# One table of 516-value rows for layer 1 of a two-layer graph attention kernel

## The chip, the cores and the metric

The kernel runs on one core of a Trainium2 chip. The metric is the device time of one execution in microseconds (us); the kernel before has a median of 4654.79 us over 3 runs (4652.91 to 4660.41). A profile was taken of a further execution.

## The reference

The inputs are 6250 nodes with 256 values each (`x`), 200,000 edges sorted by destination (`src`, `dst`) with 32 attributes each, and two layers of weights. Before the layers, each node row is normalized (`_layernorm`) and clipped at zero. One layer does the following, cut to what matters (`_gat`; `_add_self_loops` adds one edge from each node to itself, with the mean of its incoming edge features):

```python
te = relu(edge_attr @ We + be) * exp(x @ Wo + bo)[src][:, None]
hx = (x @ Wg).reshape(n, h, f)
al = leaky_relu(einsum(hx, a_s)[src] + einsum(hx, a_d)[dst] + einsum(he, a_e), 0.2)
al = exp(al - segment_max(al, dst)[dst])
al = al / segment_sum(al, dst)[dst]
out = segment_sum(hx[src] * al[:, :, None], dst) + b
```

Layer 0 has 4 heads, layer 1 has 1 head. Layer 0 is followed by a residual and a relu, layer 1 by residuals. So layer 1 needs, for any edge, the row of its source node as layer 0 left it, and layer 0 is complete only after its last edges.

## The kernel before, in words

**Steps.** The edges are cut into chunks of 128 and the chunks into 66 steps per layer (`NS`): 64 steps of 24 chunks, and two shorter ones. A step holds edges in order of destination, so its destinations are a window of at most 112 consecutive nodes (`M`), starting at a row known only at run time. The 132 steps run in one stream, unrolled, by `edges`; the last three steps of a layer are interleaved by hand in `ending`, which also starts the next layer. That place is called the turn here, and the last three steps of layer 0 are called a, b and c.

**One step.** GpSimd (POOL) issues 24 indirect DMAs (`gathers`, L1116). Each brings 128 source rows, one per partition, from the node table of the layer into a buffer `G`; there are three such buffers, so a step's gathers can start once the sums of three steps before are done. TensorE turns edge attributes into logits (`y`, `zad`); VectorE (DVE) computes logits, running maxima and weights, scales `G` (L1517), builds one-hot rows `S` (L1346); TensorE then adds up the 24 chunks into the window's nodes (`sums`, L1529: 24 products `S`ᵀ`G`, each recorded as two matmuls). `evict` (L1535) copies the sum out on ScalarE (ACT), and one to two steps later `finish`, `rows1`, `rows2` and `rows3` complete the window's nodes while the next sums run.

**Node tables.** Layer 0 gathers from `T[0]`, written in the prologue. A finished window of layer 0 gives rows `trow` of 516 values: 260 that layer 1 gathers (`L1.TW`), and 256 that layer 1 adds to its output at the end (`D`). The kernel before writes them to up to three places: the 260 values to `T[1]` (L1662), for the gathers of layer 1; for all steps before a, the same 260 values again to `T1e` (L1664); and all 516 values to a fixed place in `nd` (`rows4`, L1687), from which layer 1 loads a window's rows as `tw` (`nodes`, L1184). As a step's first node may be shared with the step before, `rows4` also patches one value in the other `nd` table (L1690).

**The turn.** While a, b and c still finish, the gathers of the first step of layer 1 already run (`early_rows` in `ending`): they read `T1e`, which holds all rows written before a. Rows that were missing then are the last 256 nodes at most. `lack_rows` loads those from `T[1]` after the stores of a, b and c (L1317), and `complete` adds them to the gathered chunks by a product with a selection matrix (L1333) on TensorE, and one VectorE operation per chunk (L1335).

**What sets the order.** SyncE's queue (SP) issues nearly all other DMAs, in program order: loads of edge attributes (`ea`), local indices (`lb`), flags (`fl`) and node rows (`tw`), and all stores. An SP instruction that waits holds up all behind it. A store to an address known only at run time is tracked as covering its whole table, so a store to `T[1]` waits until the one before has landed, a load waits for stores before it in program order, and a store waits for earlier reads. A run-time address is read by `row` with a TENSOR_LOAD into an SP register.

Of the kernel before, what the change touches and what calls it, by code (L numbers as in the profile page):

```python
# [31 lines left out]
P = 128  # L32
# [49 lines left out]
class Kernel:  # L82
# [10 lines left out]
    def run(self):  # L93
        nc, tc = self.nc, self.tc
        self.cp = self.pool("consts")
        self.dp = self.pool("tables", space=DRAM)
        N = self.N
        self.T = [self.dp.tile([N + P, L.TW], F32, name=f"T{L.l}") for L in self.L]
        self.T1 = self.dp.tile([N + P, self.L[1].TW], F32, name="T1e")
        n, w = (self.NS + 1) // 2, self.L[1].TW + D  # L100
        self.nd = [self.dp.tile([n * (M + 1), w], F32, name=f"nd{i}") for i in range(2)]
        self.x1 = self.dp.tile([N + P, D], F32, name="x1")
        with ExitStack() as c:
            c.enter_context(tc.manual_schedule())
            self.gp = [self.pool("gath0", 1, c)]
            self.ps_k = self.pool("ps_k", 1, c, space=PSUM)
            self.lp = self.pool("loads", 2, c)
            self.sp, self.wp, self.xp = (self.pool(n, b, c, side="right") for n, b in (("onehot", 2), ("work", 2), ("index", 1)))
            self.offs = offs = np.concatenate([[0], np.cumsum(self.cs)]).tolist()
            self.steps = [dict(L=L, s=s, C=self.cs[s], o=offs[s], k=L.l * self.NS + s)  # L110
                          for L in self.L for s in range(self.NS)]
            self.prologue(c)
            self.edges(c)
        self.general()
# [793 lines left out]
    def ending(self, a, b, c, pv, late, after):  # L908
# [197 lines left out]
    def gathers(self, st, behind=None):  # L1106
        nc, L = self.nc, st["L"]
        own, G = "own" in st, st.get("own")
        if not own:
            G = self.G0 if st["k"] == 0 else self.gp[st["k"] % 3].tile([P, C, 270], F32, name="G")  # L1110
        st["G"] = G
        idx = self.src[:, st["o"]:st["o"] + st["C"]]
        last = st["C"] - 1
        c0 = (self.CX, self.CX1, 0)[min(st["k"], 2)]
        for i, c in enumerate(range(last + 1) if own else (last, *range(c0, last)) if c0 <= last else ()):
            g = nc.gpsimd.indirect_dma_start(  # L1116
                out=G[:, c, 0:L.TW], out_offset=None, in_=st.get("from", self.T[L.l])[0:self.N, :],
                in_offset=bass.IndirectOffsetOnAxis(ap=idx[:, c:c + 1], axis=0))
            self.after_product(g, behind(i) if behind else None)
            yield  # L1120
# [57 lines left out]
    def nodes(self, st):  # L1178
        nc, L, s = self.nc, st["L"], st["s"]
        tw = self.tws[st["k"] % 4]  # L1180
        st["tw"], st["xw"] = tw[:, :L.TW], tw[:, L.TW:L.TW + D]
        if L.l:
            n = s // 2 * (M + 1)
            nc.sync.dma_start(tw[1:M + 1, :L.TW + D], self.nd[s % 2][n:n + M, :])  # L1184
            return
        st["r"] = r = self.row(0, s)
# [63 lines left out]
    def lacking(self):  # L1250
# [4 lines left out]
        for n in (N - 2 * P, N - P):  # L1255
            nc.sync.dma_start(self.T1[n:n + P, :], none)
        first = self.base_f[:, NS - 3:NS - 2]
# [54 lines left out]
    def lack_rows(self, st):  # L1312

        st["tail"] = [self.np_.tile([P, 272], F32, name="U", bufs=3) for _ in range(2)]
        for j, t in enumerate(st["tail"]):
            n = self.N - 2 * P + P * j
            self.nc.sync.dma_start(t[:, :self.L[1].TW], self.T[1][n:n + P, :])  # L1317

# [337 lines left out]

    def rows3(self, st):
        nc, L, s = self.nc, st["L"], st["s"]
        if L.l == 0:
            self.table_row(st)  # L1660
            r, t, L1 = st["r"], st["trow"], self.L[1]
            nc.sync.dma_start(self.T[1][ds(r, M), :], t[1:M + 1, :L1.TW])  # L1662
# [11 lines left out]
        elif s < self.direct:  # L1674
            r = self.row(1, s)
            nc.sync.dma_start(out[ds(r, M), :], o[1:M + 1, :])
# [7 lines left out]
    def rows4(self, st):  # L1684
        nc, s, t, L1 = self.nc, st["s"], st["trow"], self.L[1]
        n = s // 2 * (M + 1)
        nc.sync.dma_start(self.nd[s % 2][n:n + M, :], t[1:M + 1, :])  # L1687
        if s:
            n = self.row(2, s - 1)
# [11 lines left out]
    def general(self):  # L1701
# [4 lines left out]
        with tc.If(fl == 0):  # L1706
            with ExitStack() as c:
# [3 lines left out]
                nc.vector.memset(zero, 0.0)  # L1711
                nc.sync.dma_start(self.T[1][N:N + P, :], zero[:, :self.L[1].TW])
                for L in self.L:
                    self.general_layer(L, wp, pp)

    def general_layer(self, L, wp, pp):
# [71 lines left out]
        def nodes(n0):  # L1788
# [8 lines left out]
            if l == 0:  # L1797
# [3 lines left out]
                self.table_row(st)  # L1801
                nc.sync.dma_start(self.T[1][rows, :], st["trow"][:, :self.L[1].TW])
                nc.sync.dma_start(self.x1[rows, :], st["trow"][:, self.L[1].TW:])
# [103 lines left out]
```

## Time and profile before

| | |
|---|---|
| median of 3 runs | 4654.79 us |
| the profiled execution's own time | 4678.05 us |
| its span, first to last instruction | 4676.0 us |
| busy: TensorE matmul (PE) | 2921.0 us, 62% |
| busy: VectorE (DVE) | 2837.0 us, 61% |
| busy: ScalarE (ACT) | 534.2 us, 11% |
| busy: GpSimd (POOL) | 3002.6 us, 64% |
| mean granted TensorE clock | 0.748 |
| share of 16 DMA engines: gathers (software queue), the other DMAs of SP | 34.4%, 11.0% |
| read from HBM, written | 544.23 MB, 45.36 MB |

Times are read from the start of the span. "L1116" is line 1116 of the kernel before. In a timeline row the first column is the start, the second the duration, and the brackets at the end say how long the engine was idle ahead of it and what ended that; "issue" means that it waited for nothing that the profile shows, "remote" that the releaser isn't known. Matmul ends are modelled, so the row of a sum tells when it was issued rather than when its result stood.

### The profile page before, as it was taken

The numbers are of one execution on the slowest core, as the hardware profiler recorded it, in microseconds if no ns is written. First come the engines' busy times: TensorE is split into PE (matmuls) and PEld (weight loads), VectorE is DVE, ScalarE is ACT, GpSimd is POOL, SyncE is SP. The second block draws the span as 40 slices with busy tenths as digits, with TensorE's granted clock in tenths as the row PEclk, the third lists the DMA queues.
The fourth block names the chain that finished last, engine by engine and source line by source line (L and its number), as shares of the span: only waits on it lengthen the run. The fifth ranks groups of instructions, "written<-read, shape, count | busy, mean of one in ns | idle before, by whom it ended". The sixth has DMA issues, their size and how long they took to land.

```text
span 4676.0 us, 35049 instructions
## 1 busy us (share of the span) xinstructions
PE 2921.0 (62%) x10090; PEld 1845.5 (39%) x10090; DVE 2837.0 (61%) x6222; ACT 534.2 (11%) x1189; POOL 3002.6 (64%) x3201
## 2 busy tenths in 40 slices
PE   8766666655666656656665566566565565656656
PEld 6533433433434433433443334334343343333434
DVE  7767666666667666666675555455554554545546
ACT  5211111111111111111110000000000000000000
POOL 5566666666666666666656666666666666666664
PEclk9877777777777777778787766767767777676777
DMA  7344444444544444544444444444444444444442
GB/s 228 109 124 130 138 126 130 138 125 131 140 125 132 136 127 132 140 125 131 133 125 114 125 114 122 124 121 118 118 124 119 118 126 112 121 125 114 122 123 74
DMA packets 248234, 591.77 MB, mean 127 GB/s; under 512 B 65849, under 2 KB 105125, under 8 KB 247783
## 3 DMA queue, kind: packets, MB, share of 16 engines
q0 software_dynamic: 150048, 422.51, 34.4%
q1 hardware_dynamic: 97009, 164.82, 11.0%
q10 hardware_dynamic: 976, 2.12, 0.1%
q8 instruction: 81, 1.33, 0.1%
q14 instruction: 120, 0.98, 0.1%
HBM read 544.23 MB, written 45.36 MB: 126 GB/s over the span
## 4 chain that ended last, share of the span: by engine, by line
DVE 25%; PE 22%; issue 21%; POOL 19%; another core or an unknown queue 10%; DMA 1%; ACT 1%; DVEq 0%; POOLq 0%; ACTq 0%
POOL G L1116 18%; PE u L1529 15%; DVE G L1517 10%; DVE S L1346 3%; PE y L1218 3%; DVE lb L1242 1%; DMA G<-T,src 1%; DVE m L1467 1%; PE fin L587 1%; DVE rt L1395 1%; PE ps L587 1%; PE zad L1227 1%; DVE al L1413 1%; PE fin L1621 1%
## 5 line engine op out<-in xcount | busy, mean ns | idle before, releaser
L1116 POOL DMA_INDIRECT G<-T,src x3066 | 2931.1, 956 | 1574.2 <-issue 896.3
L1529 PE MATMUL u<-G,S 128*128 128x270 f32 (+1 forms) x6212 | 1716.8, 434 | 792.8 <-issue 567.0
L1529 PEld LDWEIGHTS u<-G,S 128*128 128x128 f32 x6212 | 1316.7, 214 | 1124.8 <-issue 609.9
L1517 DVE TENSOR_TENSOR G<-G,kps 128x6144 f32<-128x6144 f32 (+6 forms) x152 | 854.5, 5629 | 0.0
L1218 PE MATMUL y<-ea,webd 64*128 64x256 f32 (+2 forms) x1056 | 450.4, 805 | 341.1 <-issue 326.8
L1445 DVE TENSOR_TENSOR_SCAN cl<-fl,cl,lf 4x129 f32<-4x129 f32 (+1 forms) x130 | 61.1, 470 | 858.1 <-remote 730.6
L1346 DVE TENSOR_TENSOR S<-kps,loc 128x3072 f32<-128x3072 f32 (+2 forms) x136 | 438.2, 3222 | 4.6
L1227 PE MATMUL zad<-R,wea 128*64 128x384 f32 (+1 forms) x1056 | 291.7, 691 | 160.9 <-ACT R L1219 104.7
L1218 PEld LDWEIGHTS y<-ea,webd 64*128 64x128 f32 x1056 | 159.9, 284 | 493.1 <-issue 472.9
L1535 ACT ACTIVATE U<-u 128x270 f32<-128x270 f32 (+1 forms) x130 | 51.2, 394 | 1953.9 <-remote 1485.5
L1219 ACT ACTIVATE R<-y,webd 128x1024 f32<-128x1024 f32 (+3 forms) x264 | 235.6, 892 | 325.2 <-PE y L1218 166.5
L1227 PEld LDWEIGHTS zad<-R,wea 128*64 128x64 f32 x1056 | 84.5, 180 | 415.7 <-ACT R L1219 221.1
L1413 DVE TENSOR_TENSOR al<-G 128x96 f32<-128x96 f32 (+1 forms) x132 | 34.3, 260 | 240.4 <-remote 198.5
L1395 DVE STREAM_TRANSPOSE rt<-zad 128x768 f32<-128x768 f32 (+1 forms) x130 | 125.9, 968 | 24.0 <-remote 20.4
L587 PE MATMUL fin<-wg,h1T 128*128 128x260 f32 x264 | 122.8, 613 | 1.5 <-issue 1.1
L1435 PE MATMUL lf<-ident,fb 128*36 128x128 f32 (+1 forms) x132 | 46.5, 353 | 120.5 <-issue 80.9
L1367 PE MATMUL zad<-a,Q 128*128 128x12 bf16 (+1 forms) x132 | 24.3, 184 | 153.6 <-issue 117.2
L1242 DVE TENSOR_TENSOR lb<-lb,kps 128x1536 bf16<-128x1536 bf16 (+1 forms) x68 | 113.0, 1661 | 0.0
L1621 PE MATMUL fin<-ident,fb 128*128 128x128 f32 x132 | 45.6, 395 | 95.4 <-issue 94.7
L1621 PEld LDWEIGHTS fin<-ident,fb 128*128 128x128 f32 x132 | 25.2, 194 | 166.0 <-issue 163.6
L1560 ACT ACTIVATE mw<-mw,mg 128x2 f32<-128x2 f32 x66 | 19.7, 298 | 595.2 <-DVE mw L1556 469.7
L1399 DVE TENSOR_REDUCE ade<-rt 128x96 f32<-128x288 f32 (+1 forms) x132 | 44.2, 335 | 70.2 <-remote 35.3
(267 smaller groups left out, 2310.1 us busy)
## 6 DMA issues: line engine op xcount, KB each, us to landing
ea<-in_ea_dram SPq DMA_DIRECT2D x64, 768.0 KB
G<-T,src POOLq DMA_INDIRECT x3066
lb<-locrow SPq DMA_DIRECT2D x64, 384.0 KB
nd<-t1rows SPq DMA_DIRECT2D x66, 225.8 KB
tw<-nd SPq DMA_DIRECT2D x66, 225.8 KB
tw<-T SPq DMA_DIRECT2D x66, 117.2 KB
T<-t1rows SPq DMA_DIRECT2D x66, 113.8 KB
tw<-in_x_dram SPq DMA_DIRECT2D x66, 112.0 KB
```

The lines of the kernel that those rows point to most:

```text
L587: self.product = self.nc.tensor.matmul(ps[:, :L.MW], hT[:, k, :], self.wg[L.l][:, k, :], start=(k == 0), stop=(k == 1))
L1116: g = nc.gpsimd.indirect_dma_start(out=G[:, c, 0:L.TW], out_offset=None, in_=st.get("from", self.T[L.l])[0:self.N, :], in_offset=bass.Indi ...
L1218: nc.tensor.matmul(y[:, i, :n], self.webd[l][r, :], ea[r, w], start=True, stop=True)
L1219: nc.scalar.activation(R[:, :, w], y[:, :, :n], AF.Relu, bias=self.be[l])
L1227: nc.tensor.matmul(st["zad"][i * PH:(i + 1) * PH, o], self.wea[l][0], R[:, i, w], start=True, stop=False)
L1242: V.tensor_tensor(lb[:, :, :n], lb[:, :, :n], self.k_part.unsqueeze(2).to_broadcast([P, i, n]), op=OP.is_equal)
L1346: nc.vector.tensor_tensor(st["S"][:, c0:c1, :], self.k_iota.unsqueeze(1).to_broadcast(w), self.loc[:, o + c0:o + c1].unsqueeze(2).to_broad ...
L1395: V.transpose(rv[:, :32 * c].rearrange("p (b n) -> p b n", b=2), z.rearrange("p (b n) -> p b n", b=2)[:, :, :16 * c])
L1413: V.tensor_add(zv, gr, G[:, :c, L.p:L.p + H])
L1517: nc.vector.tensor_tensor(v, v, pw[:, c0:c1, :].unsqueeze(3) .to_broadcast([P, c1 - c0, H, L.F]), op=OP.mult)
L1529: p = nc.tensor.matmul(st["u"][:, :L.W], S[:, i, :], G[:, i, 0:L.W], start=(j == 0), stop=(j == c - 1))
L1621: st["turned"] = self.nc.tensor.transpose(pT[:, i * P:(i + 1) * P], st["x1"][:, i * P:(i + 1) * P], self.ident)
```

## The change

`T[1]` becomes a table with rows of 516 values. `T1e` is gone.

- In layer 0, a step before a to c stores all 516 values of a window to `T[1]` in one DMA (`store_row`), except that `nd` is still written for the last four steps of the layer, which read it in layer 1. The copy to `T1e`, the store to `nd` and its patch are gone for the others.
- Gathers of layer 1 read the first 260 values of a 516-value row; there are as many of them, in the same order, with 260 values each.
- In layer 1, the first 62 steps load `tw` from `T[1]` at the window's row; the row is read into a register there and used again for the store of the output, where it was read before.
- The early gathers read `T[1]` itself. So that they see no half-written rows, a's rows are stored after the last early gather in program order; by the tracking of the whole table, this store waits until all 24 early gathers have landed. The stores of a, b and c carry 260 values each, as before.

```diff
-        self.T1 = self.dp.tile([N + P, self.L[1].TW], F32, name="T1e")
         n, w = (self.NS + 1) // 2, self.L[1].TW + D
+        self.T = [self.dp.tile([N + P, (L.TW, w)[L.l]], F32, name=f"T{L.l}") for L in self.L]
...
-            after["from"] = self.T1
...
-            self.rows3(a)
+            self.rows3(a, not early)
         self.rows1(b)
         if early:
             self.product = b["turned"]
             drain(early_rows)
+            self.store_row(a)
         self.rows2(b)
...
-        if L.l:
+        if L.l and s + 4 >= self.NS:
             n = s // 2 * (M + 1)
             nc.sync.dma_start(tw[1:M + 1, :L.TW + D], self.nd[s % 2][n:n + M, :])
             return
+        if L.l:
+            st["r"] = r = self.row(1, s)
+            nc.sync.dma_start(tw[1:M + 1, :L.TW + D], self.T[1][ds(r, M), :])
+            return
...
+    def store_row(self, st):
+        r, t, w = st["r"], st["trow"], self.L[1].TW + (0 if "lag" in st else D)
+        self.nc.sync.dma_start(self.T[1][ds(r, M), 0:w], t[1:M + 1, :w])
...
-            nc.sync.dma_start(self.T[1][ds(r, M), :], t[1:M + 1, :L1.TW])
-            if self.early and s + 3 < self.NS:
-                nc.sync.dma_start(self.T1[ds(r, M), :], t[1:M + 1, :L1.TW])
-            if "lag" not in st:
+            if store:
+                self.store_row(st)
+            if "lag" not in st and s + 4 >= self.NS:
                 self.rows4(st)
```

The order of instructions on PE, DVE, ACT and POOL is the same but for the table that the early gathers name. SP's changes. In a step of layer 0, SP's stores of the kernel before are these (the names are the destination and the source; `T1_61` is `T[1]`):

```order
L1662 DMA T1_61<-t1rows_202 112x260
L1664 ISA
L1664 DMA T1e_62<-t1rows_202 112x260
L1687 DMA nd1_64<-t1rows_202 112x516
L1175 TENSOR_LOAD base_i_1264
L1690 ISA
L1690 DMA nd0_63<-t1rows_202 1x1
```

The kernel after has one store there, and goes on to the next loads:

```order
L1142 DMA lb_9990<-locrow_1207 128x1x1536
L1142 DMA ea_10063<-in_ea_dram 128x2x768
L1663 ISA
L1663 DMA T1_61<-t1rows_201 112x516
L1174 TENSOR_LOAD base_i_1263
```

Four DMAs became one, of the size of the largest.

At the turn, SP of the kernel before issues the stores of a, b and c (L1662), the two loads of the missing rows and the first `tw` of layer 1. The names in brackets are the semaphores that the instruction waits for: DMAHW ones count DMAs of SP, DMASW ones the gathers of POOL, the others their engine.

```order
L1662 DMA T1_61<-t1rows_202 112x260 [waits DMAHW3_49,Activation_49]
L1662 ISA
L1662 DMA T1_61<-t1rows_202 112x260 [waits DMAHW4_49,DMAHW3_49,Activation_49]
L1662 DMA T1_61<-t1rows_202 112x260 [waits DMAHW5_49,DMAHW4_49,Activation_49]
L1317 DMA U_12565<-T1_61 128x260 [waits DMAHW6_49,DMAHW5_49,Pool_49]
L1317 DMA U_12566<-T1_61 128x260 [waits DMAHW7_49]
L1184 DMA tw4_203<-nd0_63 112x516 [waits DMAHW0_49]
```

In the kernel after the same place reads:

```order
L1663 DMA T1_61<-t1rows_201 112x260 [waits DMASW4_49,DMASW5_49,DMASW3_49,DMASW6_49,DMASW2_49,DMASW7_49,DMASW1_49,DMAHW4_49,DMASW0_49,Activation_49]
L1663 ISA
L1663 DMA T1_61<-t1rows_201 112x260 [waits DMAHW2_49,Activation_49]
L1663 DMA T1_61<-t1rows_201 112x260 [waits DMAHW3_49,Activation_49]
L1321 DMA U_12193<-T1_61 128x260 [waits DMAHW5_49,DMAHW4_49,Pool_49]
L1321 DMA U_12194<-T1_61 128x260 [waits DMAHW6_49]
L1174 TENSOR_LOAD base_i_1263 [waits DVE_49]
L1187 ISA
L1187 DMA tw4_202<-T1_61 112x516 [waits DMAHW7_49]
```

The first store waits for all eight semaphores of the gathers; the stores of b and c, the loads of the missing rows and the first `tw` are queued behind it.

In a step of layer 1, SP of the kernel before has the row's register load ahead of the output's store:

```order
L1184 DMA tw4_203<-nd0_63 112x516
L1143 DMA lb_14948<-locrow_1208 128x1x1536
L1143 DMA ea_15006<-in_ea_dram 128x2x768
L1175 TENSOR_LOAD base_i_1264
L1676 ISA
L1676 DMA out_0_dram<-fb_14938 112x256
```

The kernel after has it ahead of the `tw` load:

```order
L1174 TENSOR_LOAD base_i_1263
L1187 ISA
L1187 DMA tw4_202<-T1_61 112x516
L1142 DMA lb_14342<-locrow_1207 128x1x1536
L1142 DMA ea_14400<-in_ea_dram 128x2x768
L1682 ISA
L1682 DMA out_0_dram<-fb_14329 112x256
```

The register load moved from the store to the load; the number of DMAs per step is the same.

More of the change, by code (lines that the diff above doesn't have):

```diff
@@ L1116, in gathers @@
             g = nc.gpsimd.indirect_dma_start(
-                out=G[:, c, 0:L.TW], out_offset=None, in_=st.get("from", self.T[L.l])[0:self.N, :],
+                out=G[:, c, 0:L.TW], out_offset=None, in_=self.T[L.l][0:self.N, :],
                 in_offset=bass.IndirectOffsetOnAxis(ap=idx[:, c:c + 1], axis=0))
@@ L1674, in rows3 @@
         elif s < self.direct:
-            r = self.row(1, s)
+            r = st["r"] if "r" in st else self.row(1, s)
             nc.sync.dma_start(out[ds(r, M), :], o[1:M + 1, :])
```

15 lines of the change are left out of this document (7 added, 8 removed).

## The prediction

> **What bounds the kernel now.** I began with the page: the chain that ended last and the costliest groups.
>
> ```profile
> span 4676.0 us, 35049 instructions
> DVE 25%; PE 22%; issue 21%; POOL 19%; another core or an unknown queue 10%; DMA 1%; ACT 1%; DVEq 0%; POOLq 0%; ACTq 0%
> L1116 POOL DMA_INDIRECT G<-T,src x3066 | 2931.1, 956 | 1574.2 <-issue 896.3
> ```
>
> No engine holds the whole chain: VectorE, TensorE and GpSimd each have about a fifth or a quarter, and DMAs 1%. That is the mark of a loop that passes through several engines. So I took the big scaling of `G`, one per step, to count steps (its rows in two stretches, one per layer), and then the timeline of one step in the middle of layer 1.
>
> ```profile
> L1517 DVE TENSOR_TENSOR G<-G,kps x57: 6545/6545/6546, 314.6 to 2282.7; 128x6144 f32<-128x6144 f32 x57
> L1517 DVE TENSOR_TENSOR G<-G,kps x55: 6545/6545/6546, 2663.9 to 4528.2; 128x6144 f32<-128x6144 f32 x55
> 3016.14 10.83 PE L1529 MATMUL u<-G,S 128*128 128x261 f32 x48 [1.84 <-issue]
> 3040.64 0.39 ACT L1535 ACTIVATE U<-u 128x261 f32<-128x261 f32 x1 [19.99 <-remote]
> 3040.67 0.47 DVE L1445 TENSOR_TENSOR_SCAN cl<-fl,cl,lf 1x129 f32<-1x129 f32 x1 [9.91 <-remote]
> 3035.56 0.95 POOL L1116 DMA_INDIRECT G<-T,src  x1 [0.30 <-issue]
> 3040.87 0.95 POOL L1116 DMA_INDIRECT G<-T,src  x1 [4.37 <-remote]
> ```
>
> A step of layer 0 takes (2282.7 − 314.6) / 56 = 35.14 us, one of layer 1 (4528.2 − 2663.9) / 54 = 34.52 us. Within a step, 24 products start at 3016.14 and their result is copied out at 3040.64, 24.5 us later. Then, in the same third of a microsecond, VectorE leaves an idle stretch of 9.91 us and GpSimd one of 4.37 us: both waited for the sums. VectorE's serial part (maxima, weights, scaling) takes the other 34.52 − 24.5 = 10.0 us. GpSimd's 24 gathers take 24 × (0.95 + 0.30) = 30.0 us, so it has 4.4 us to spare. The loop is sums, VectorE, sums; gathers come next, 4.4 us behind. The waits say what gathers and stores cost this loop:
>
> ```profile
> PE u L1529 <- DMA G<-T,src: 16.1, 7, 3.1
> POOL G L1116 <- DMA T<-t1rows: 4.8, 1, 4.8
> PE y L1333 <- DMA U<-T: 3.9, 1, 3.9
> ```
>
> Products wait for gathered rows 16.1 us in the whole execution, in 7 places. The other two waits happen once each: at the turn.
>
> **Layer 0: four DMAs become one.** In the chain, and in the timeline of a step of layer 0:
>
> ```profile
> 2395.36 0.05 DVEq L592
> 1517.81 0.41 DVE L592 TENSOR_TENSOR t1rows<-fin,bias 128x260 f32<-128x260 f32 x1
> 1517.93 11.70 PE L1529 MATMUL u<-G,S 128*128 128x270 f32 x42 [2.83 <-DVE crow L1505]
> 1542.02 0.40 ACT L1535 ACTIVATE U<-u 128x270 f32<-128x270 f32 x1 [10.94 <-PE u L1529]
> ```
>
> About 62 steps lose the copy to `T1e`, the store to `nd` and the patch. No engine of the loop issues them, SP does. What they could hold up is the reuse of their source `t1rows`: L592 writes it at 1517.81, while the step's sums start at 1517.93 and stand at 1542.02, so VectorE has 24.1 us of cover there. The one wait that the chain shows for L592 is 0.05 us. So the term is 0; without cover it would be 0.05 us × 62 = 3 us gained. The other end is the whole difference between the layers, (35.14 − 34.52) × 62 = 38 us gained, if the stores' traffic were all of what makes a step of layer 0 longer. Layer 0 does other work in its steps (a running maximum of four heads against one, rows of the next layer), which explains a difference of 0.6 us as well, and the small share of DMA waits speaks for it. I take 0 and keep the gain as a rival.
>
> **Layer 1: gathers from wider rows.** Each gather still brings 128 × 260 values, but from rows 2064 bytes apart instead of 1040. No row of before has such a stride. The durations of all gathers so far:
>
> ```profile
> L1116 POOL DMA_INDIRECT G<-T,src x3066: 943/949/1174, 89.5 to 4630.8; - x192
> ```
>
> [...] I take 0. The other end is 1174 − 949 = 225 ns more for each, the worst that the row shows; that is a rival below. A gain here isn't excluded by a row, but GpSimd isn't the bound, so it would be worth nothing beyond the 16.1 us of landings.
>
> **Layer 1: the load of `tw`.** It now comes from `T[1]` at a run-time row, and the register is loaded ahead of it. The timeline of the same step, and the register work for the loads of layer 0, which are at a run-time row already (from the `tw` tile's rows):
>
> ```profile
> 3022.70 0.44 DVE L1643 SCALAR_TENSOR_TENSOR fb<-tw,mw,fb 128x256 f32<-128x256 f32 x1
> 3023.18 0.32 SPq L1184 DMA_DIRECT2D tw<-nd  x1
> 3026.45 0.17 DVE L1359 CAST a<-tw 128x2 bf16<-128x2 f32 x1
> L1187 SPq MOVE tw<-in_x_dram x66: 29/705/1442, 92.9 to 2337.1; - x66
> ```
>
> The load is issued when L1643 has read the place before it, 3.3 us ahead of its reader L1359. Register work ahead of such a load cost SP at most 1.4 us each (the MOVE's maximum). All of that would push L1359, the work up to the idle stretch with it, and use 1.4 of the 9.91 us that VectorE waits there anyway. So 0, with the cover named: the wait for the sums. If the cover were gone, 1.4 × 62 = 87 us; it would have to shrink seven times for that. The output's store needs its register no longer there, a gain off the path.
>
> **The turn.** Here the change adds a wait. The timeline of before around it (SP's queue, POOL, PE):
>
> ```profile
> 2398.39 11.29 SPq L1662 DMA_DIRECT2D T<-t1rows  x3
> 2406.34 0.94 POOL L1116 DMA_INDIRECT G<-T1e,src  x1 [0.30 <-issue]
> 2409.36 0.32 SPq L1662 DMA_DIRECT2D T<-t1rows  x1
> 2411.35 0.84 SPq L1317 DMA_DIRECT2D U<-T  x2
> 2412.24 0.43 SPq L1184 DMA_DIRECT2D tw<-nd  x1
> 2412.09 0.95 POOL L1116 DMA_INDIRECT G<-T,src  x1 [4.81 <-DMA T<-t1rows]
> 2413.64 0.77 PE L1333 MATMUL y<-U,G 128*128 128x260 f32 x1 [3.92 <-DMA U<-T]
> L1662 SPq EVENT_SEMAPHORE  x2: 1562/1882/2203, 2399.2 to 2402.2; - x2
> L1317 SPq EVENT_SEMAPHORE  x1: 1590/1590/1590, 2409.7 to 2409.7; - x1
> ```
>
> Before, the rows of a and b are stored from 2398.39 on, while the early gathers still run; only c's store at 2409.36 stands at the end, and has landed by 2411.3, when SP, after its wait of 1590 ns, goes on to the loads of the missing rows. After, a's store waits for the last early gather. That is issued by 2406.34 + 0.94 = 2407.28, and lands 1.6 to 2.2 us later if it takes as long as the stores (SP's waits for a store: 1562 to 2203 ns): 2408.9 to 2409.5. Behind a's store, in SP's queue, are the stores of b and c, each waiting for the one before, the loads of the missing rows, and the first `tw`. Three stores one after another, 0.33 us to issue and 1.6 to 1.9 us to land each, are 5.8 to 6.6 us: c lands at 2414.7 to 2416.1 instead of 2411.3. That is +3.4 to +4.8 us; I take the upper half, **+4.2 us**, as SP also goes through more semaphores there. Both who wait are shifted by it: PE's L1333 (its wait of 3.92 us becomes about 8.1) and GpSimd's first gather of the second step of layer 1 (4.81 becomes 9.0). Nothing hides it, as the first scaling of layer 1 needs all 24 chunks completed. The first `tw` of layer 1, at 2412.24, is shifted by as much plus at most 1.4 us; its reader L1359 comes at 2425.45, 13 us after the issue, and is shifted itself, so that stays covered.
>
> What a longer idle stretch does to the clock is the open part. Three stretches after the turn (busy time with counts of PE, PEld, DVE, ACT, POOL, then the granted clock), with rows of the timeline:
>
> ```profile
> 2413.40:2416.80 3.40, 3.16 (x7) 2.52 (x8) 2.58 (x4) 0.00 (x0) 2.79 (x3) 0.50 0.68 192
> 2416.80:2423.60 6.80, 3.90 (x18) 3.14 (x17) 3.28 (x8) 0.00 (x0) 4.97 (x6) 1.00 0.60 168
> 2423.60:2430.40 6.80, 3.90 (x12) 1.55 (x12) 1.97 (x8) 0.00 (x0) 5.28 (x6) 0.50 0.54 138
> 2425.45 0.15 DVE L1359 CAST a<-tw 128x1 bf16<-128x1 f32 x1
> 2426.23 0.16 PE L1367 MATMUL zad<-a,Q 128*128 128x3 bf16 x1 [5.54 <-issue]
> 2446.89 0.48 DVE L1335 SCALAR_TENSOR_TENSOR G<-G,known,fin 128x260 f32<-128x260 f32 x1 [0.39 <-PE fin L1333]
> 2447.76 0.48 DVE L1335 SCALAR_TENSOR_TENSOR G<-G,known,u 128x260 f32<-128x260 f32 x1 [0.39 <-PE u L1333]
> ```
>
> The clock is 0.50 after TensorE's idle 3.92 us, full 3.4 us later, and 0.50 again about its idle 5.54 us. So before already pays the fall that a wait can cause, and I add nothing for a longer one; the ends are 0 and one more stretch of 3.4 us at half speed, 1.7 us lost. [...]
>
> **Sum.** 0 + 0 + 0 + 4.2 us. The execution profiled has a time of 4678.05 us and would have 4682.2; the median of the runs lies 23.3 us lower, and with the same term 4654.8 + 4.2 = 4659.0 us. About 0.2%, 9.3 us, is what a measurement of this kernel can tell from no change; 4.2 us is less.
>
> **Rivals.** *B, faster by the traffic saved.* A step of layer 0 writes 113.8 + 113.8 + 225.8 KB and now 225.8 KB, and SP has fewer waits ahead of its loads:
>
> ```profile
> nd<-t1rows SPq DMA_DIRECT2D x66, 225.8 KB
> T<-t1rows SPq DMA_DIRECT2D x66, 113.8 KB
> ```
>
> If half of the 38 us goes with them, the time is 4654.8 − 19 + 4.2 = 4640 us. For it: the steps of layer 0 are longer by 0.62 us, and a late gather reaches TensorE at once. Against it: only 16.1 us of waits for gathers, in 7 places. [...] Chance 0.18.
>
> *C, slower by the gathers.* GpSimd has 4.37 us to spare per step of 24 gathers, so it becomes the bound from 4.37 / 24 = 0.18 us more per gather. At 0.225 us more (the maximum above) a step takes 24 × (0.949 + 0.304 + 0.225) = 35.5 us instead of 34.52, over 64 steps +61 us: 4720 us with the turn. Against it: the instruction's size and its count of indices are the same. Chance 0.07.
>
> *D, slower by the clock at the turn.* The last two rows of `complete` above are 2447.76 − 2446.89 = 0.87 us apart, at the full clock; at 0.50 it is 1.74. If the longer idle stretch leaves TensorE at 0.50 through the later 18 of the 24 chunks, that is 18 × 0.87 = 15.7 us, and the time 4654.8 + 4.2 + 15.7 = 4675 us. It decides from 6 such chunks on (5.2 us, which with 4.2 us passes 9.3). For it: the clock falls twice in this very place. Against it: it was back at 1.00 within 3.4 us of work after the wait of before. Chance 0.11.
>
> That the change doesn't do what it says is no rival here: the order of instructions shows one store per step, and a's store with waits on all eight semaphores of the gathers.
>
> **How the numbers follow.** The forecast, with all else hidden, has the remaining 0.64. Its own range is 4652 to 4666 us: at the lower end 3 us are gained on `t1rows` and the turn costs 3.4 us, less the 2 us by which the runs shown fall below their median; at the upper end the turn costs 4.8 us and the clock 1.7, and the runs scatter upwards by 5 us. Over 0.2% faster (below 4645.5) is B but for its smallest effects, 0.17, and a little of the forecast's tail: 0.2. Over 0.2% slower (above 4664.1) are C and D, 0.18, and a little of the other tail: 0.2. The rest is 0.6. The range has to leave out no more than 2 in 10: it goes down to 4636, half of B's gain (19 us) in full with no loss at the turn, and up to 4670, into D; left out are C, the upper half of D and the outer part of B.
>
> **What the profile after would show.** Right: scaling of `G` in steps of 35.1 and 34.5 us as before; gathers of 949 ns in the median in layer 1; the first store of a with a wait of some 7 to 10 us on SP behind the last early gather; PE's first product of `complete` idle for about 8 us ahead of it, and the first gather on `T[1]` behind it after about 9 us on GpSimd. Wrong: steps of layer 0 shorter by 0.3 us or more (B); gathers over 1.13 us, with no idle time of GpSimd left (C); 24 chunks of `complete` all near 1.7 us apart (D); VectorE waiting for a `tw` load at L1359 in layer 1.

## The result, and the profile after

In 20 runs of each, the changed kernel has a median of 4651.23 us (4647.52 to 4659.90) and the kernel before one of 4656.46 us (4652.51 to 4663.07). The ratio is 0.9986, interval 0.9980 to 0.9992: some 6.5 us faster (5.2 us between the medians), where 4.2 us slower had been forecast. The size is inside the bound of 0.2% that the prediction set for "same", but the sign is the other one, and the interval leaves no room for +4.2 us (1.0009).

The two profiled executions differ by more: 4678.05 us before, 4650.5 after. The first lies above all 20 timed runs of its kernel, so that the spans are not simply subtracted below; a second profile of before was taken for that. Of the changed kernel, the page's span, chain and gathers (mean of one: 954 ns, before 956):

```profile
span 4648.4 us, 34562 instructions
DVE 38%; PE 19%; another core or an unknown queue 16%; issue 16%; POOL 9%; DMA 1%; ACT 1%; DVEq 0%; SPq 0%; POOLq 0%; ACTq 0%
L1115 POOL DMA_INDIRECT G<-T,src x3090 | 2947.4, 954 | 1587.1 <-issue 896.3
```

The scaling of `G`, one per step, now L1521, in the stretches of layer 0 and layer 1:

```profile
L1521 DVE TENSOR_TENSOR G<-G,kps x57: 6545/6545/6546, 312.5 to 2256.8; 128x6144 f32<-128x6144 f32 x57
L1521 DVE TENSOR_TENSOR G<-G,kps x58: 6545/6545/6546, 2605.9 to 4571.0; 128x6144 f32<-128x6144 f32 x58
```

A step of layer 0 takes (2256.8 − 312.5) / 56 = 34.72 us, where the first profile of before had 35.14; one of layer 1 takes (4571.0 − 2605.9) / 57 = 34.48, where it had 34.52. So layer 1 is as forecast and layer 0 isn't. A part of layer 0's difference between these two executions is that products wait less for gathered rows, first before and then after (382 to 2270 us; total, times and longest wait):

```profile
PE u L1529 <- DMA G<-T,src: 13.9, 6, 3.1
PE u L1533 <- DMA G<-T,src: 1.4, 1, 1.4
```

The turn, by the timeline of SP's queue, GpSimd and TensorE and by SP's waits:

```profile
SPq L1663 <- DMA G<-T,src: 6.0, 1, 6.0
2383.14 4.10 SPq L1663 DMA_DIRECT2D T<-t1rows  x3
2388.85 0.84 SPq L1321 DMA_DIRECT2D U<-T  x2
2389.58 0.94 POOL L1115 DMA_INDIRECT G<-T,src  x1 [8.74 <-DMA T<-t1rows]
2391.19 2.07 PE L1337 MATMUL y<-U,G 128*128 128x260 f32 x4 [7.24 <-DMA U<-T]
```

The parts are those of the forecast, with one smaller: the store of a waits 6.0 us on SP for the early gathers (forecast 7 to 10), the three stores follow one another, GpSimd waits 8.74 us (before 4.81, forecast 9.0) and TensorE 7.24 (before 3.92, forecast 8.1). The loss at the turn is there; something else gains more.

### The profile page after: what moved, and what is told of

Its sections match the earlier page's. It is cut to its first block, busy times and chain, and to the rows that moved or that the text cites. A ratio compares the mean times of both kernels' runs of the same rounds, so it can differ in the third digit from the quotient of the medians.

```text
span 4648.4 us, 34562 instructions
## 1 busy us (share of the span) xinstructions
PE 2924.5 (63%) x10090; PEld 1838.4 (40%) x10090; DVE 2832.6 (61%) x6222; ACT 532.6 (11%) x1189; POOL 2995.7 (64%) x3201
## 4 chain that ended last, share of the span: by engine, by line
DVE 38%; PE 19%; another core or an unknown queue 16%; issue 16%; POOL 9%; DMA 1%; ACT 1%; DVEq 0%; SPq 0%; POOLq 0%; ACTq 0%
DVE G L1521 13%; PE u L1533 12%; POOL G L1115 9%; DVE S L1350 5%; PE y L1221 3%; DVE lb L1245 1%; DVE rt L1399 1%; DVE m L1471 1%; DVE al L1417 1%; DVE al L1419 1%; DMA G<-T,src 1%; PE fin L586 1%; DVE al L1421 1%; DVE a3r L1364 1%
## 5 line engine op out<-in xcount | busy, mean ns | idle before, releaser
L1533 PE MATMUL u<-G,S 128*128 128x270 f32 (+1 forms) x6212 | 1691.6, 430 | 694.3 <-issue 486.5
L1521 DVE TENSOR_TENSOR G<-G,kps 128x6144 f32<-128x6144 f32 (+6 forms) x152 | 854.5, 5630 | 0.0
L1221 PE MATMUL y<-ea,webd 64*128 64x256 f32 (+2 forms) x1056 | 460.8, 816 | 369.7 <-issue 354.7
L1385 PE MATMUL zad<-lb,aq 128*128 128x384 bf16 (+2 forms) x264 | 84.7, 413 | 0.0
```

The source lines that it names most:

```text
L1221: nc.tensor.matmul(y[:, i, :n], self.webd[l][r, :], ea[r, w], start=True, stop=True)
L1385: self.nc.tensor.matmul(st["zad"][:, o], st["aq"].rearrange("p k j -> p (k j)"), st["lb"][:, w], start=False, stop=True)
L1521: nc.vector.tensor_tensor(v, v, pw[:, c0:c1, :].unsqueeze(3) .to_broadcast([P, c1 - c0, H, L.F]), op=OP.mult)
L1533: p = nc.tensor.matmul(st["u"][:, :L.W], S[:, i, :], G[:, i, 0:L.W], start=(j == 0), stop=(j == c - 1))
```

## Experiments

The experiments ran in six jobs, each a set of runs on one chip, and each job had another chip. The kernel before took 4618 to 4620 us in the first two, 4022 to 4024 us in the next two, 4670 and 4614 us in the last two. Each ratio below is against the kernel before in the same job. Two theories of the gain in layer 0 stood against each other: *queue*, that the removed instructions had stood ahead of the loads of node rows in SP's queue, and *stores*, that the DMAs or their bytes cost time as such.

### Before and after again

Both kernels without an edit.

> The kernel before, unchanged, to have a second profile of it, since the first profiled execution took 4678 us where the median of 20 runs is 4656.5. Every theory expects 4656 us and a ratio of 1.000; the open point is where the second profile is shorter. If the 21 us lie in layer 0's steps (35.13 us on average in the first profile, 34.70 in the changed kernel), then most of the difference between the two profiles is chance, and the steps come out near 34.8.

> The changed kernel, unchanged, on this job's chip, with a second profile. By the first comparison (20 runs each) the ratio is 0.9986, some 6.5 us below the kernel before. If the gain of layer 0's stores belongs to a chip or an execution on which gathers land late (13.9 us of waits of the products in layer 0 in the first profile of before, 1.0 us in the second), the gain is gone here: the turn's loss is left, ratio 1.0005 to 1.0015, with steps of layer 0 of 34.4 us as before has them. If it is SP's queue or the stores' bytes as such, the ratio is again 0.9986 and the steps of layer 0 are shorter than those of before by 0.15 us or more.

Before: 0.9999 (0.9989 to 1.0008). After, in the second job: 0.9996 (0.9987 to 1.0005), which can't be told from no change. The same scaling, from the sixth step to the last ahead of the turn (56 rows, 55 steps), and then to the first full step behind it (15 rows); first before, then after:

```profile
L1517 DVE TENSOR_TENSOR G<-G,kps x56: 6544/6545/6546, 381.5 to 2276.1; 128x6144 f32<-128x6144 f32 x56
L1517 DVE TENSOR_TENSOR G<-G,kps x15: 415/2277/6546, 2276.1 to 2513.4; 128x6144 f32<-128x6144 f32 x5, 128x256 f32<-128x256 f32 x3, 128x2048 f32<-128x2048 f32 x2, 128x2304 f32<-128x2304 f32 x1
```

```profile
L1521 DVE TENSOR_TENSOR G<-G,kps x56: 6544/6545/6546, 381.1 to 2272.9; 128x6144 f32<-128x6144 f32 x56
L1521 DVE TENSOR_TENSOR G<-G,kps x15: 414/2278/6546, 2272.9 to 2514.8; 128x6144 f32<-128x6144 f32 x5, 128x256 f32<-128x256 f32 x3, 128x2048 f32<-128x2048 f32 x2, 128x2304 f32<-128x2304 f32 x1
```

The 55 steps take 1894.6 and 1891.8 us, the turn 237.3 and 241.9 us: 2.8 us less and 4.6 us more, on two chips of nearly the same time. A step of layer 0 of before takes 34.45 us here, not 35.13. So most of the 0.42 us per step between the first two profiles belongs to that execution of before, not to the change, as the 5 us between the medians also say.

What could the queue do? In before, of the same two kernels, the load of a node row (SP's timeline), its reader on VectorE, L1359, which runs in every second step, the instruction behind the reader, the copied-out sums (ACT) and the first scan of the maxima, which comes right behind them:

```profile
1542.57 0.71 SPq L1188 DMA_DIRECT2D tw<-T  x1
1545.12 0.17 DVE L1359 CAST a<-tw 128x8 bf16<-128x8 f32 x1
1546.84 0.17 DVE L1360 TENSOR_TENSOR a3r<-tw,a 128x8 f32<-128x8 f32 x1 [1.55 <-remote]
1547.15 0.40 ACT L1535 ACTIVATE U<-u 128x270 f32<-128x270 f32 x1 [11.80 <-PE fin L1621]
1547.34 0.47 DVE L1445 TENSOR_TENSOR_SCAN cl<-fl,cl,lf 4x129 f32<-4x129 f32 x1
L1445 DVE TENSOR_TENSOR_SCAN cl<-fl,cl,lf 4x129 f32<-4x129 f32 x55 | 25.9, 470 | 6.7 <-PE zad L1367 4.9 <-PE lf L1435 0.8
L1445 DVE TENSOR_TENSOR_SCAN cl<-fl,cl,lf 1x129 f32<-1x129 f32 x57 | 26.9, 471 | 810.5 <-remote 454.3 <-PE y L1218 356.2
```

The last two rows are the groups of that scan in layer 0 and in layer 1. In layer 1 VectorE idles 810.5 / 57 = 14.2 us right ahead of it per step; in layer 0 6.7 / 55 = 0.12 us. That isn't all of its slack in layer 0: between the load's reader and the scan it idles at L1360, 1.55 us here. Over the 27 steps with that reader (382 to 2280 us):

```profile
DVE a3r L1360 <- remote: 35.5, 18, 2.9
DVE a3r L1360 <- DVE a L1359: 4.8, 8, 0.9
```

That is 40.3 us, 1.5 us in every second step. The load that VectorE reads at 1545.12 has been issued 1545.12 − 1543.28 = 1.84 us before; this is called its margin. L1359 has no idle time ahead of it: it doesn't wait for the load, here or anywhere else between 382 and 2280 us in either profile of before. After:

```profile
1532.07 0.70 SPq L1191 DMA_DIRECT2D tw<-T  x1
1541.64 0.17 DVE L1363 CAST a<-tw 128x8 bf16<-128x8 f32 x1
```

The margin is 1541.64 − 1532.77 = 8.87 us here.

### Stores put back, stores doubled

```diff
 # changed kernel: all old stores back in layer 0
+            if s + 3 < self.NS:
+                nc.sync.dma_start(self.T1[ds(st["r"], M), :], st["trow"][1:M + 1, :self.L[1].TW])
-            if "lag" not in st and s + 4 >= self.NS:
+            if "lag" not in st:
                 self.rows4(st)
...
-        if s and s + 3 >= self.NS:
+        if s:
```

> The changed kernel with the three removed DMAs put back into each step of layer 0 (copy of 260 values, 516 values to the fixed place, the patch), which nothing reads for the steps concerned. If the gain is layer 0's stores (theory S: about 9 us gained there, 2.5 us lost at the turn), the time goes to 4656.5 + 2.5 = 4659 us, ratio 1.0005. If the gain lies in layer 1 (theory L: the load of the node rows, the shorter work of SP there), it stays at about 4651 us, ratio 0.9987. If half and half, 4655.

1.0009 (1.0000 to 1.0018), where theory S named 1.0005, theory L 0.9987: with the stores back no gain is left, which points to layer 0. The changed kernel itself has 0.9996 in the second job, and the two intervals overlap.

```diff
 # kernel before: three more DMAs per step of layer 0
+                nc.sync.dma_start(self.T2[ds(r, M), :], t[1:M + 1, :L1.TW])
...
+            nc.sync.dma_start(self.ne[s % 2][n:n + M, :], t[1:M + 1, :])
+            n = self.row(2, s - 1)
+            nc.sync.dma_start(self.ne[(s - 1) % 2][ds(n, 1), L1.ad:L1.ad + 1], t[1:2, L1.ad:L1.ad + 1])
```

> The kernel before with three more DMAs in each step of layer 0, of the same sizes as the three that the change removes, into tables that nothing reads. Theory S expects the same again, about +9 us: 4665 us, ratio 1.0019, or more if SP's queue becomes full. Theory L expects no change, 4656 us.

1.0110 (1.0094 to 1.0125), +51 us: far over the 9 us expected, and the waits of layer 0 show a new one, on the load of node rows, in 26 places (and one on gathers, which before had 1.0 us in this stretch):

```profile
DVE a L1361 <- DMA tw<-T: 78.8, 26, 4.4
PE u L1531 <- DMA G<-T,src: 25.2, 10, 3.1
```

### Bytes alone, instructions alone

```diff
 # bytes: two more stores of 516 values at fixed places
+            for i in range(2):
+                nc.sync.dma_start(self.ne[2 * i + s % 2][n:n + M, :], t[1:M + 1, :])
 # instructions: two more patches of one value at run-time rows
+            for i in range(2):
+                n = self.row(2, s - 1)
+                nc.sync.dma_start(self.ne[2 * i + s % 2][ds(n, 1), L1.ad:L1.ad + 1], t[1:2, L1.ad:L1.ad + 1])
```

> The kernel before with two more stores of 516 values in each step of layer 0 (451.6 KB, at fixed places, without register work: two more instructions on SP). If the 51 us that the doubled stores cost (339.6 KB) are a matter of bytes beside the gathers, this costs more than those, about +68 us. If they come from SP's queue, which issues the load of the node rows later, then only the two instructions count, 1.4 to 2.8 us of delay against a margin of 1.2 to 3.2 us between that load and its reader: +0 to +25 us.

> The kernel before with two more patches of one value in each step of layer 0, each with its register load: some eight more instructions on SP, 8 bytes. Theory queue: as much as the doubled stores, about +50 us, VectorE waiting for the load of the node rows in every second step. Theory bytes: no change, ratio 1.000.

Bytes: 1.0002 (0.9993 to 1.0011). Instructions: 1.0100 (1.0085 to 1.0115), +46 us. The waits of layer 0 with the patches, and one of the 26 places in VectorE's timeline with the load's issue:

```profile
DVE a L1360 <- DMA tw<-T: 84.4, 26, 4.6
1504.40 0.34 SPq L1189 DMA_DIRECT2D tw<-T  x1
1504.72 0.40 ACT L1536 ACTIVATE U<-u 128x270 f32<-128x270 f32 x1 [11.12 <-PE fin L1622]
1506.55 0.18 DVE L1360 CAST a<-tw 128x8 bf16<-128x8 f32 x1 [3.07 <-DMA tw<-T]
1507.27 0.47 DVE L1446 TENSOR_TENSOR_SCAN cl<-fl,cl,lf 4x129 f32<-4x129 f32 x1
```

VectorE waits 3.07 us for the load, and the scan that follows stands 1507.27 − 1504.72 = 2.55 us behind the copied-out sums instead of 0.19 in the row of before above. 451.6 KB more per step cost nothing that can be measured; 8 bytes with their register work cost 46 us. The 40.3 us of idle time at L1360 are gone in the run with the patches; 84.4 us of waits less 40.3 us of idle time that they use up are 44 us, close to the 46. So VectorE's slack behind the load, 1.5 us in every second step, is what the added instructions had to exceed.

On this chip the bytes cost nothing measurable (1.0002), against the traffic of rival B. It isn't tested on the chip of the first comparison, the only one where a profile of before shows products waiting long for gathers in layer 0 (13.9 us; the second profile 1.0).

### The loads moved ahead in the queue

```diff
 # kernel before, and kernel before with the two more patches
-            if self.early and s + 3 < self.NS:
-                nc.sync.dma_start(self.T1[ds(r, M), :], t[1:M + 1, :L1.TW])
             if "lag" not in st:
-                self.rows4(st)
+                self.copies = st
...
                     self.nodes(q)
+            if getattr(self, "copies", None):
+                self.copies_of(self.copies)
+                self.copies = None
```

`copies_of` issues the copy, the fixed-place store and the patches. First with the two patches, in two jobs, the first of them on a chip of the 4022 us kind.

> The kernel before with the two more patches that cost 46 us, but with the loads of the node rows issued ahead of the copy, the fixed-place store and all three patches. Theory queue: the 46 us are gone, ratio 0.999 to 1.001, and no wait of VectorE for the load is left. Theory that the instructions cost as such (SP full): still +46 us, ratio 1.010. On a chip on which a step is bound by GpSimd's 30.1 us, both expect no change.

> As the run before of the same kernel: two more patches per step of layer 0 (which cost 46 us behind their place in SP's queue), with the loads of the node rows issued ahead of them. Where a step of layer 0 takes 34.4 us: theory queue 0.999 to 1.001 and no wait of VectorE for the load; theory that the instructions cost as such 1.010. Where GpSimd bounds the step, no change, as measured.

0.9997 (0.9988 to 1.0006), and in the second job, where the kernel before took 4670 us, 1.0013 (1.0004 to 1.0022). There +6 us instead of +46, and no wait for the loads of node rows is left. What waits now in layer 0 is the load of the edge attributes, which stands behind the patches:

```profile
ACT t1rows L1637 <- DMA ea<-in_ea_dram: 27.2, 5, 6.0
1488.07 0.71 SPq L1192 DMA_DIRECT2D tw<-T  x1
1494.19 0.26 DVE L1363 CAST a<-tw 128x8 bf16<-128x8 f32 x1
```

So the cost of the added instructions is, for the greater part, their place in the queue; the 46 us and the 6 us come from different chips. Then the same move in the kernel before itself:

> The kernel before with the same DMAs, but in layer 0 SP issues the next loads of node rows (x and the table row) ahead of the copy, the fixed-place store and the patch instead of behind them. Theory queue (the removed instructions matter because they stand ahead of those loads): the evict-to-maxima gap of VectorE and the margin of the loads become those of the changed kernel and the gain in layer 0 comes without any store removed, 4 to 9 us, ratio 0.998 to 0.9991. Theory stores (the DMAs or bytes as such): no change, ratio 1.000.

> The kernel before with the same DMAs, the loads of node rows ahead of the copy, the fixed-place store and the patch in SP's queue. Where a step of layer 0 takes 34.4 us or more: theory queue 0.998 to 0.9991 (4 to 10 us less), the loads 5 us or more ahead of their reader, and VectorE's maxima 0.2 us behind the copied-out sums instead of 0.33 to 0.65; theory stores 1.000 and a gap as before. Where GpSimd bounds the step, no change, as measured.

0.9999 (0.9990 to 1.0008) on the 4024 us kind, 1.0001 (0.9992 to 1.0011) where before took 4614 us. In the second, the margin is what the changed kernel has, and the 55 steps take 2275.0 − 380.9 = 1894.1 us, where the second profile of before, on another chip, has 1894.6:

```profile
1534.72 0.71 SPq L1191 DMA_DIRECT2D tw<-T  x1
1545.67 0.17 DVE L1362 CAST a<-tw 128x8 bf16<-128x8 f32 x1
L1520 DVE TENSOR_TENSOR G<-G,kps x56: 6543/6545/6546, 380.9 to 2275.0; 128x6144 f32<-128x6144 f32 x56
```

10.24 us bring nothing more than 1.84. Here the theory queue missed: it explains what added instructions cost, but at the size of the change itself no gain from the place alone could be measured. The margin is no sharp measure either. In the run of bytes alone it falls to 1550.45 − 1550.01 = 0.44 us by the same rows, and the reader doesn't wait:

```profile
1549.30 0.71 SPq L1189 DMA_DIRECT2D tw<-T  x1
1550.45 0.17 DVE L1360 CAST a<-tw 128x8 bf16<-128x8 f32 x1
```

One more patch, a half of that load on the queue, ran in two jobs, both on the 4022 us kind:

> The kernel before with one more patch of one value per step of layer 0 (four SP instructions, 2.8 to 5.6 us later loads), half of what cost 46 us. Theory queue: a threshold, since the loads of the node rows are issued 1.2 to 3.2 us ahead of their reader in every second step and take some 1.1 to 1.8 us: VectorE begins to wait, +10 to +30 us. If each instruction cost the same, +23 us; if the cost comes from the whole queue being full, 0.

> One more patch per step of layer 0, as before. Where a step takes 34.4 us: theory queue +10 to +30 us, with VectorE waiting for the load of the node rows in every second step; in proportion +23 us. Where a step is bound by GpSimd's 30.1 us: no change, as measured.

0.9997 (0.9988 to 1.0006) and 1.0001 (0.9992 to 1.0010). It tells nothing on threshold or price per instruction where a step takes 34.4 us.

### The turn alone, the wide table alone

```diff
 # kernel before with the turn of the changed kernel
-            after["from"] = self.T1
...
-            self.rows3(a)
+            self.rows3(a, not early)
...
             drain(early_rows)
+            self.store_row(a)
```

> The kernel before with the turn of the changed kernel alone: the early gathers read the table itself and the rows of a are stored after them; all stores stay. My prediction's term: +4.2 us, 4660.7 us; the two profiles show 2.5 us more from the last steps of layer 0 to the first of layer 1, which gives 4659. A rival, that the gain comes from the turn (other clock, other order of loads), expects about 4650.

1.0022 (1.0012 to 1.0032), +8 us by the medians: a loss, and a larger one than the 1.0009 forecast. Its profile has 6.5 us more in the stretch around the turn than that of before in the same job (243.8 against 237.3 us).

```diff
 # changed kernel: all old stores back as above, early gathers from a copy, a stored in its old place
+            after["from"] = self.T1
```

> The wide table alone: layer 1 gathers from 516-value rows and loads its node rows from them, as in the changed kernel, while layer 0 keeps all its stores (nothing reads the fixed places for these steps) and the turn is that of before, with its own copy for the early gathers. My prediction's terms for both are 0: ratio 1.000. The runs with the stores put back and with the turn alone differ by 2.3 us in favour of the first, so the other expectation is 0.9995.

1.0007 (0.9998 to 1.0016): no gain from the wide table or the loads from it. The changed kernel ran in the same job and differs from this one by the old stores and the turn alone. Its median is 4618.5 us against 4623.8, 5.3 us less although it has the longer turn, and its 55 steps of layer 0 take 1891.8 us against 1896.1. So leaving out the old stores gained several us there too.

### Where GpSimd bounds the step

> The changed kernel again, beside the others. Its ratio was 0.9986 (0.998 to 0.9992) on the first chip and 0.9996 (0.9987 to 1.0005) on the second. If both saw the same effect, 0.999; if the gain exists only where before's gathers land late, 1.000; where GpSimd bounds the step, the stores cannot matter and the turn's loss is left, 1.0005 to 1.001.

> The changed kernel with the turn of before: the rows of a are stored where before stores them, and the early gathers read the table of layer 0 instead, so that nothing waits (the chunks of the first step of layer 1 then hold other rows than the reference's). Left is the gain in layer 0 without the loss at the turn. With the turn at +3.3 to +4.6 us by the profiles so far and the changed kernel at -1.5 us on this kind of chip, the ratio should be 0.9986 to 0.999; if the turn costs what the run of the turn alone showed (+7.8), 0.998; if the turn costs nothing in the end, 0.9996.

> A version that might beat both: the changed kernel with the copy of 260 values kept for the early gathers alone, so that the turn is that of before; layer 0 then has two stores per step, no fixed place and no patch. Theory queue: two SP instructions more than the changed kernel leave the margin of the loads at 5 us or more, nothing is lost in layer 0, and the ratio is that of the run with the turn undone, 0.998 to 0.999. Theory stores: part of the gain is lost again, 0.9993 or above.

> The changed kernel with the copy of 260 values kept for the early gathers, turn as before. Where a step takes 34.4 us: below the changed kernel by the turn's 3 to 5 us, ratio 0.998 to 0.999. Where GpSimd bounds the step: the same difference from the changed kernel, as the turn is there as well.

```diff
 # changed kernel: turn of before; early gathers from a copy (or, turn undone, from self.T[0])
+            after["from"] = self.T1
...
-            self.rows3(a, not early)
+            self.rows3(a)
...
-            self.store_row(a)
...
+            if self.early and s + 3 < self.NS:
+                nc.sync.dma_start(self.T1[ds(st["r"], M), :], st["trow"][1:M + 1, :self.L[1].TW])
```

On the 4022 us kind, the changed kernel is slower: 1.0017 (1.0008 to 1.0026), +6.8 us by the ratio. With the turn undone, which leaves the first step of layer 1 without its right source rows, it is 0.9993 (0.9984 to 1.0002), with the copy kept 0.9995 (0.9986 to 1.0004) and 0.9994 (0.9985 to 1.0003). The scaling of `G`, and the first gather from the full table on GpSimd, first in the changed kernel and then with the copy kept:

```profile
L1521 DVE TENSOR_TENSOR G<-G,kps x56: 6544/6545/6547, 320.8 to 1978.3; 128x6144 f32<-128x6144 f32 x56
L1521 DVE TENSOR_TENSOR G<-G,kps x15: 414/2277/6545, 1978.3 to 2182.3; 128x6144 f32<-128x6144 f32 x5, 128x256 f32<-128x256 f32 x3, 128x2048 f32<-128x2048 f32 x2, 128x2304 f32<-128x2304 f32 x1
2071.30 0.94 POOL L1115 DMA_INDIRECT G<-T,src  x1 [8.75 <-DMA T<-t1rows]
```

```profile
L1523 DVE TENSOR_TENSOR G<-G,kps x56: 6545/6545/6547, 320.5 to 1975.0; 128x6144 f32<-128x6144 f32 x56
L1523 DVE TENSOR_TENSOR G<-G,kps x15: 414/2278/6546, 1975.0 to 2169.1; 128x6144 f32<-128x6144 f32 x5, 128x256 f32<-128x256 f32 x3, 128x2048 f32<-128x2048 f32 x2, 128x2304 f32<-128x2304 f32 x1
2063.92 0.94 POOL L1116 DMA_INDIRECT G<-T,src  x1 [3.53 <-DMA T<-t1rows]
```

A step of layer 0 takes 1657.5 / 55 = 30.14 us and 1654.5 / 55 = 30.08: GpSimd's 24 gathers, each 0.95 us and 0.30 us to the next in its timeline, are 24 × 1.25 = 30.0 us. Nothing is left for layer 0 to gain, and the wait at the turn, now on the engine that sets the step, costs 204.0 − 194.1 = 9.9 us from the last step ahead of the turn to the first behind it. The version with the copy kept is the changed kernel without that loss. It is faster than the changed kernel there by some 8 us (the two intervals don't meet), and can't be told from before.

## Why the prediction was wrong, step by step

**The turn: right in its parts, a little off in size.** +4.2 us was forecast. On the chips where before takes 4614 to 4620 us, the stretch around the turn takes 237.3 to 241.1 us in six profiles with the turn of before (mean 239.0) and 241.7 to 243.8 us in three with the new one (mean 242.5): 3.5 us more. In whole runs the turn alone cost some 8 us, at least 5.5 by its interval; the rest of that isn't explained. Where GpSimd bounds the step, the same wait costs 8 to 10 us.

**Layer 1: right.** Gathers of 955 ns on average in layer 1 (median 946, from 2580 to 4600 us), steps of 34.48 us, no wait for `tw`; the wide table alone is 1.0007.

**The clock at the turn (rival D) and slower gathers (rival C): did not come.** After the longer wait, the first three chunks of `complete` in the changed kernel start 1.7 to 1.9 us apart (2391.19, 2393.06, 2394.79, 2396.53), the next ones 0.9. The granted clock is 0.50 from 2391.19 to 2394.60, 0.69 from there to 2398.00 and 1.00 in the 3.4 us behind that. Before has two such gaps there, 1.9 and 1.5 us, and also a clock of 0.50 behind its shorter wait (2413.40 to 2416.80); so the longer wait added one chunk at the slower pace, about 1 us, within the 1.7 us that the prediction allowed. What sets the time of a gather no run shows, and the 0 for the wider rows was the author's estimate; the gathers of layer 1 took 946 ns in the median from rows of 516 values, and 949 from rows of 260 in the same stretch of before.

**Layer 0: wrong.** The step that failed is "So the term is 0", with its sentence on what the removed DMAs could hold up, "the reuse of their source `t1rows`". To account for a ratio of 0.9986 with a loss of some 4 us at the turn, layer 0 has to gain about 10 us; beside the wide table alone it gained several us as well. Two things were missed. The removed instructions hold up what is queued behind them on SP, the loads of node rows among it: with them such a load was issued 1.84 us ahead of its reader, without them 8.87 us, in the rows above. And the cover that was named, 24.1 us of sums, is a stretch of TensorE: VectorE's own idle time between such a load's reader and the maxima is 1.5 us in every second step. The experiments show both for added instructions: two more patches in that place cost 46 us, which is their 84.4 us of waits less the 40.3 us of idle time, and with the loads moved ahead some 6 us are left (on another chip). They don't show that the removal gains by the same way.

**Rival B had the sign, in part by luck.** It named the traffic saved and SP's fewer waits ahead of its loads, with 19 us of gain. Its sign, steps of layer 0 shorter by 0.3 us or more, is there in the first pair of profiles (0.42 us), most of which belongs to one execution, and not in the second (34.45 against 34.40 us).

**What stays open.** Why the removal gains time in layer 0 is not shown. A wait for the loads of node rows is not it as far as the traces go: in both profiles of before their reader never waits in that stretch, so a margin of 8.87 us had no wait to remove. Moving the loads alone, at the size of the change, gave 1.0001 where before took 4614 us. Late gathers may have a part on the first chip (13.9 us of waits against 1.4); 451.6 KB more per step made no difference (1.0002), but on another chip, and that a store lengthens a gather beside it no run shows. Other loads behind the removed stores may matter too, as the edge attributes did in one run (27.2 us of waits). The size is open as well: the intervals of 0.9986 and 0.9996 overlap, and a common value near 0.999 would fit both, but not the 1.0017 of the chip on which GpSimd is the bound.

## What to carry to other kernels

Price an instruction on a DMA queue by what is queued behind it: for each load there, take the time from its issue to its reader, and count the idle time of the reader's engine behind it in that very stage, as the slack of another layer says nothing (here 14.2 us per step in layer 1, and 1.5 us in every second step of layer 0). Here a delay cost about what exceeded that idle time (46 us, where 84.4 us of waits stood against 40.3 us of idle time), and earlier loads gained nothing measurable where their reader had not waited (1.0001). So ask of a removed instruction which wait it ends, and find that wait in the trace, before giving it a gain. A loss at one place and a gain spread over a stage need not keep their sum: where GpSimd bounded the steps, the gain was gone and the loss at the turn larger (1.0017 against 0.9986; 9.9 us at the turn, against a mean of 3.5 us where before takes 4614 to 4620 us).

## What the runs showed of the hardware

The same kernel took 4670, 4656, 4614 to 4620 and 4022 to 4024 us in different jobs, by far more than any edit here. The stretch of the sums shows where the two kinds part. Of one step of layer 1, the 24 products and the copy of their result, in the second profile of before and in the changed kernel on the 4022 us kind:

```profile
3000.01 12.52 PE L1529 MATMUL u<-G,S 128*128 128x261 f32 x48 [2.04 <-DVE G L1507]
3024.55 0.39 ACT L1535 ACTIVATE U<-u 128x261 f32<-128x261 f32 x1 [20.04 <-PE y L1218]
3006.00:3012.00 6.00, 6.00 (x29) 5.15 (x28) 2.15 (x9) 0.00 (x0) 4.47 (x6) 1.00 0.67 155
3012.00:3024.00 12.00, 2.96 (x9) 1.35 (x7) 0.00 (x0) 0.00 (x0) 6.54 (x7) 0.61 0.42 116
```

```profile
3022.25 10.83 PE L1533 MATMUL u<-G,S 128*128 128x261 f32 x48 [0.86 <-DVE G L1511]
3033.11 0.39 ACT L1539 ACTIVATE U<-u 128x261 f32<-128x261 f32 x1 [6.36 <-PE u L1533]
3020.00:3030.00 10.00, 9.14 (x39) 6.82 (x38) 8.80 (x17) 0.30 (x1) 7.56 (x8) 0.91 0.39 105
```

The copy starts 24.5 us after the first product in one and 10.9 us in the other. The products themselves differ little: their rows span 12.5 us against 10.8, and the granted clock (third number from the end in the rows of the stretches) is 1.00 in the later half of the slower ones. What differs is the time from there to the copy, 12.0 us against none. In it TensorE is busy for 2.96 us with 9 matmuls, the last of the products among them, GpSimd issues 7 gathers, and the granted clock is 0.61; whether that clock and the late copy have to do with each other the rows don't say. Why the copy comes so late on the one kind isn't shown: matmul ends are modelled, so the rows don't say when the sums stood. The prediction put all 24.5 us down to the sums. The step is set by this stretch on the one kind and by GpSimd on the other, so that the same edit has another price on each.
